# Half of the token tiles loaded in transposed form, their layer norm applied after the transposition by GpSimd, in a two-level fast matrix product

## Chip, core and metric

The kernel runs on one core of a Trainium2 chip. A core has TensorE (PE, matrix products into PSUM banks), VectorE (DVE), ScalarE (ACT), GpSimd (POOL) and SyncE (SP), which issues nearly all transfers here. Each engine takes its instructions in order; waits between engines are semaphores. The metric is the device time of one execution in microseconds (us).

## What is computed

2048 tokens of 512 features, two weight paths on the same normalised tokens, all float32:

```python
xn = (x - mean(x)) / sqrt(var(x) + eps)                  # per token
s  = xn @ (weight * block_mask).T                        # 512 -> 512
nx = xn * rsqrt(mean(xn**2) + eps) * ln_w
g  = silu( (silu(nx @ gate_w.T) * (nx @ up_w.T)) @ down_w.T )   # 512 -> 1792 -> 512
out = x + s * g
```

## The kernel before

**Two levels of a seven-product scheme.** Every matrix product is cut into 2 x 2 blocks twice, and at each level eight block products are replaced by seven, at the price of sums of blocks (Winograd's form of Strassen's scheme). For the first product the token operand B is xn transposed, features on the partitions: four chunks c of 128 features by four tiles t of 512 tokens. Chunk c = 2K + k and tile t = 2H + n, where (K, H) is the outer block and (k, n) the inner one. `raw[c, t]` is such a 128x512 tile. From the outer blocks come the seven outer operands q (`outer_b`):

- q = 1, 2, 3 are the blocks B(0,0), B(1,0), B(1,1) themselves,
- q = 5 is B(0,1) - B(0,0), q = 6 is B(1,1) minus operand 5, q = 7 is B(1,1) - B(0,1), q = 4 is B(1,0) minus operand 6.

`inner_b` makes four inner sums of each in the same way. The weight operand is cut and summed in parallel (`inner_a`, on GpSimd: four sums of 128x256 for the two first q of a group, four of 128x640 for the other five). There are eight weight groups: seven of gate and up columns and, as g = 7, the masked weight.

**Order by hand.** Every step is put down with `at(position, function, ...)`; at the end (L877) all are emitted in order of position. A position is one 128x512 product on TensorE, two records in the trace. An instance, one (g, q), has seven products and starts at 7j, j being its number; neighbouring instances overlap a little. First come q = 1 and 2 for all eight groups (positions 0 to 112): they need only tiles 0 and 1, the first half of the tokens. From position 112 on come the other five q of each group, which need tiles 2 and 3 too; after them the down projection (`down_instance`, L591). PSUM banks are shared out by letter: X (3), Y (2) and Z (1) for products, V (2) for everything else: transposes, gates, rows.

**The second half of the tokens**, in positions 14 to 82, beside the products of the first half:

- All four token tiles are loaded in natural form (tokens on the partitions, `load_x`) at the very start.
- `stats` (DVE, L125 and L126) takes mean and variance of each 128 tokens: tile 2 from position 14, tile 3 from 25.
- `factors` makes the scale and the bias per token, in three steps: DVE, a square root on ScalarE (L140), DVE (L136, L137). Those of tiles 2 and 3 stand at positions 36 to 38.5, beside those of `rms_factor`.
- `normalise` applies them in place: tile 3 on DVE (L146), tile 2 on ScalarE (L148).
- 32 TensorE transposes (`transpose`, L155) in eight batches of four, from position 51.5 for tile 3 and 65.5 for tile 2, into V banks.
- Chunks 2 and 3 (K = 1) are copied out by ScalarE (`evacuate`, L163). Chunks 0 and 1 (K = 0) stay in their bank and are read from there by DVE for the outer sums q = 5 and 7. DVE also makes q = 6; GpSimd makes q = 4, at positions 78 to 82.

**Queues.** SP issues its transfers in order of position as well: token loads, weight loads (`load_a`, `load_block`), stores of the hidden activations to `h_dram`, of partial sums to `acc_dram`. A transfer that must wait for its data holds back those behind it. Near the end `load_final` reads each tile of x transposed once more, for the residual sum.

The schedule of the steps named, in the kernel's own lines:

```python
    for t, p, step in ((0, T(7.1), 0), (1, T(12.5), 0), (2, 36.0, 1.2), (3, 36.1, 1.2)):
        plan(p, step, factors(t))
...
        at(14.0 + 2.5 * i, stats, 2, i)
        at(25.0 + 3 * i, stats, 3, i)
        at((44.0, 51.0, 55.2, 58.2)[i], normalise, 2, i, act)
        at(40.5 + 2.4 * i, normalise, 3, i, dve)
```

Of the kernel before, what the change touches and what calls it, by code (L numbers as in the profile page):

```python
# [8 lines left out]
F32 = mybir.dt.float32  # L9
I32 = mybir.dt.int32  # L10
AF = mybir.ActivationFunctionType
ALU = mybir.AluOpType
AX = mybir.AxisListType

P = 128
W = 512
# [15 lines left out]
def tile_masked_linear_gated_ffn(  # L32
# [11 lines left out]
    nc = tc.nc  # L44
    NT, H = x.shape
    KC = H // P
    G = gu.shape[0]
    NTT = NT // W
    TT = W // P
# [2 lines left out]
    h_dram = tc.dram_tile([7, G, 2, P, W], F32, name="h_dram")  # L52
    s_dram = tc.dram_tile([KC, NTT, P, W], F32, name="s_dram")
    rms_dram = tc.dram_tile([NT], F32, name="rms_dram")
    acc_dram = tc.dram_tile([G + 1, P, 4, W], F32, name="acc_dram")
    dw_dram = tc.dram_tile([4, P, G, 256], F32, name="dw_dram")

    const = ctx.enter_context(tc.tile_pool(name="const", bufs=1))
    small = ctx.enter_context(tc.tile_pool(name="small", bufs=2))
# [8 lines left out]
    def at(pos, fn, *args):  # L68
        events.append((pos, len(events), fn, args))
# [5 lines left out]
    mem = big.tile([P, sum(n for _, n in RINGS), W], F32, tag="mem", name="mem")  # L75
# [5 lines left out]
    F = first_slot  # L81

    def slot(tag, name=None):
        i, n = ring[tag]
        ring[tag][0] += 1
        return mem[:, first_slot[tag] + i % n, :]
# [6 lines left out]
    def bank(tag, name):  # L93
        return ps.tile([P, W], F32, tag=tag, name=name, bufs=PSB[tag])

    def add(eng, o, a, b, op=ALU.add):
        eng.tensor_tensor(o, a, b, op)  # L97

    dve, pool, act = nc.vector, nc.gpsimd, nc.scalar
# [3 lines left out]
    ident = const.tile([P, P], F32, tag="ident", name="ident")  # L103
# [9 lines left out]

    xt, raw, stat = {}, {}, {}
    agg = small.tile([P, NTT, TT, 2], F32, tag="agg", name="agg", bufs=1)
    rms = small.tile([P, NTT, TT], F32, tag="rms", name="rms", bufs=1)

    def load_x(t):
# [9 lines left out]
    def factors(t):  # L128


        scl = small.tile([P, TT], F32, tag="scl", name=f"scl_{t}")
        nb = small.tile([P, TT], F32, tag="nb", name=f"nb_{t}")
        stat[t] = (scl, nb)

        def last():
            nc.vector.reciprocal(scl, scl)  # L136
            nc.vector.scalar_tensor_tensor(nb, agg[:, t, :, 0], -1.0, scl, ALU.mult, ALU.mult)  # L137

        return [lambda: nc.vector.tensor_scalar(scl, agg[:, t, :, 1], 1.0 + EPS, EPS * EPS, ALU.mult, ALU.add),
                lambda: nc.scalar.activation(scl, scl, AF.Sqrt), last]  # L140
# [9 lines left out]
    pt = {}  # L150
# [17 lines left out]
    def rms_factor():  # L168

        def first():  # L170
            nc.vector.tensor_scalar_add(rms, agg[:, :, :, 1], EPS)
            nc.vector.reciprocal(rms, rms)
            nc.vector.tensor_mul(rms, agg[:, :, :, 1], rms)
            nc.vector.tensor_scalar_add(rms, rms, EPS)
        return [first, lambda: nc.scalar.activation(rms, rms, AF.Sqrt)]

    def rms_store():

        b = bank("V", "rms_rows")
        nc.tensor.transpose(b[: NTT * TT, :P], rms.rearrange("p t i -> p (t i)"), ident)  # L180
        rows = small.tile([NTT * TT, P], F32, tag="rms_rows", name="rms_rows", bufs=1)
        nc.vector.tensor_copy(rows, b[: NTT * TT, :P])
        nc.sync.dma_start(rms_dram.rearrange("(i p) -> i p", p=P), rows)

# [4 lines left out]
        nc.sync.dma_start(rms_bc[t], rms_dram[t * W : (t + 1) * W].unsqueeze(0).to_broadcast([P, W]))  # L189


    bblk, bop = {}, {}

    def outer_b(q, k, n, eng):


        B = lambda K, H_: pt[2 + n, k] if (K, H_) == (0, 1) else raw[2 * K + k, 2 * H_ + n]
        if q in (1, 2, 3):
            bblk[q, k, n] = B(*{1: (0, 0), 2: (1, 0), 3: (1, 1)}[q])
            return  # L200
        o = mem[:, F["free"], :] if (q, k, n) == (4, 0, 1) else slot("tmp" if (k, n) == (0, 1) else f"B{q}")
        a, b = {
            5: lambda: (B(0, 1), B(0, 0)),
            6: lambda: (B(1, 1), bblk[5, k, n]),
            7: lambda: (B(1, 1), B(0, 1)),
            4: lambda: (B(1, 0), bblk[6, k, n]),
        }[q]()
        add(eng, o, a, b, ALU.subtract)
        bblk[q, k, n] = o

    def inner_b(q, m, eng):
# [344 lines left out]
    fin, at_later = {}, []  # L556

    def load_final(R, Hh, i, slot_s, slot_x):
        r, n = divmod(i, 2)
        t, m = 2 * Hh + n, 2 * R + r  # L560
        fin[m, t] = mem[:, slot_s, :], mem[:, slot_x, :]
        nc.sync.dma_start(fin[m, t][0], s_dram[m, t])
        s_tile = fin[m, t][0]
        at_later.append(lambda: nc.gpsimd.tensor_tensor(s_tile, s_tile, rms_bc[t], ALU.mult))  # L564
        nc.sync.dma_start(fin[m, t][1], x_t[m * P : (m + 1) * P, t * W : (t + 1) * W])

    def finish(R, Hh, i, y, pos, eng, part=slice(0, W), source=None):
        r, n = divmod(i, 2)
# [108 lines left out]
    T = lambda us: (us - 14.0) / 0.86  # L677
# [17 lines left out]
    def plan(pos, step, todo):  # L695
        for i, fn in enumerate(todo):
            at(pos + step * i, fn)


    def warm(n, b):  # L700
        for _ in range(n):
            nc.tensor.matmul(b[:, :P], ident, ident, start=True, stop=True, skip_group_check=True)

    at(T(1.4), lambda: warm(26, bank("V", "idle")))
    for t, p, step in ((0, T(7.1), 0), (1, T(12.5), 0), (2, 36.0, 1.2), (3, 36.1, 1.2)):
        plan(p, step, factors(t))
    for i in range(TT):
        half = act if i < 2 else dve
# [16 lines left out]
    for q in (1, 2):  # L725
        for k in (0, 1):
            for n in (0, 1):
                at(8, outer_b, q, k, n, None)
    at(2.1, scale_a, 1, 0)
    at(5.2, scale_a, 1, 1)  # L730
    for i in range(TT):
        at(14.0 + 2.5 * i, stats, 2, i)
        at(25.0 + 3 * i, stats, 3, i)
        at((44.0, 51.0, 55.2, 58.2)[i], normalise, 2, i, act)
        at(40.5 + 2.4 * i, normalise, 3, i, dve)
    plan(36.2, 1.2, rms_factor())

    for t, p0 in ((3, 51.5), (2, 65.5)):
        n = t % 2
        for k, c in enumerate((2, 3, 0, 1)):  # L740
            for i in range(TT):
                at(p0 + 2 * k + 0.01 * i, transpose, t, c, i, "V")
            if c >= 2:
                at(p0 + 2 * k + 1.2, evacuate, t, c, act)
            else:
                at(p0 + 2 * k + 1.2, outer_b, 5, c, n, dve)
                at(p0 + 2 * k + 1.21, outer_b, 7, c, n, dve)
    for k in (0, 1):
        for n in (0, 1):
            at(72, outer_b, 3, k, n, None)  # L750
    for n, p0 in ((1, 60), (0, 74)):
        for k in (0, 1):
            at(p0 + 1.5 * k, outer_b, 6, k, n, dve)
            at(p0 + 2.2 + 1.7 * k + (16 if n == 1 else 4), outer_b, 4, k, n, pool)
    for q, p in ((6, 77), (5, 83), (4, 89), (7, 100), (3, 118)):
        for off, m, eng in ((0, 5, dve), (3, 6, dve), (5.5, 7, pool), (7.5, 4, pool)):
            at(p + off, inner_b, q, m, eng)
# [3 lines left out]
    for g in range(G + 1):  # L761
        p, rest = 7 * where[g, 1], 7 * where[g, BLOCKS[0]]
# [27 lines left out]
    for i, (R, K) in enumerate(QUADS):  # L790
        at(50, load_mask, R, K)
        at(62 + 3.5 * i, mask_rows, R, K)
    at(79.5, mask_blocks)
    at(120, rms_store)
    for t in range(NTT):
        at(END + 13, rms_rows, t)
# [51 lines left out]
    for (R, Hh), pos in (((0, 0), [D(0)(16)] * 4), ((1, 1), [D(2)(8)] * 4),  # L848
                         ((0, 1), [D(4)(20), D(4)(24), D(5)(3), D(5)(7)]),
                         ((1, 0), [D(5)(18), D(5)(22), D(6)(1), D(6)(5)])):  # L850
        for i, p in zip((0, 3, 1, 2), pos):
            at(p, load_final, R, Hh, i, fin_slots[0][i], fin_slots[1][i])
            at(p + 9, lambda: at_later.pop(0)())
# [71 lines left out]
```

## Time and profile before

| | us |
|---|---|
| median of three runs | 513.16 (512.6 to 513.7) |
| profiled execution | 513.17 |
| its span, first to last instruction | 511.4 |
| TensorE busy | 505.8 |
| VectorE busy | 380.4 |
| GpSimd busy | 340.9 |
| ScalarE busy | 182.6 |

The granted TensorE clock was 1.0 throughout. The mean traffic was 238 GB/s. In the stretch that the change touches, from 26 to 78 us, GpSimd is busy 11.5 us, VectorE 41.4 and ScalarE 34.3 of 52.

How to read it: a line of the table of groups or of an answer names the source line, the engine, the operation, its output and inputs, and then busy time, mean and waits. L97 is the line of a helper that makes every elementwise sum, so its groups are told apart by tiles and shapes. A line of waits reads "engine and line that waited <- what ended the wait: us in total, times, the longest". A line of a timeline reads "start, length, engine, line, operation, output<-inputs, shape, how many".

### The profile page before, as it was taken

To read this page: it belongs to the slowest core of one execution; us is meant where nothing else is said; L and a number is where in the kernel's file an instruction comes from. 1 tells how busy PE (TensorE), PEld (TensorE's weight loads), DVE (VectorE), ACT (ScalarE), POOL (GpSimd) and SP (SyncE) were. 2 spreads that over 40 slices of the span, in tenths; PEclk is the share of its full clock that TensorE was granted. 3 is DMA by queue.
4 is the path that set the end of the run, shared out by engine and by line. 5 is a ranking of instruction groups with operands and counts; after the bars stand their busy time and mean duration, and the time that the engine had idled before them with its cause. 6 is when DMAs were issued, how large, how long until landed. Compare 5 with 4: busy or idle time off the path is not lost. (4 is left out here: it accounts for less than half of the span.)

```text
span 511.4 us, 4943 instructions
## 1 busy us (share of the span) xinstructions
PE 505.8 (99%) x1269; PEld 231.8 (45%) x1269; DVE 380.4 (74%) x590; ACT 182.6 (36%) x348; POOL 340.9 (67%) x283
## 2 busy tenths in 40 slices
PE   8999999999999999999999999999999999999997
PEld 8444444444444444444444444444444444444444
DVE  6878689876977969699696978968747645367736
ACT  4656754633536353353634433330100101001111
POOL 5522224994795968869597789976662754739960
PEclk9999999999999999999999999999999999999999
DMA  8436636369159386785948667499997698476472
GB/s 289 164 132 238 247 133 227 135 236 350 48 219 348 147 302 228 238 289 208 338 166 294 209 239 254 169 332 383 357 339 270 204 374 327 146 252 216 151 229 83
DMA packets 60460, 121.59 MB, mean 238 GB/s; under 512 B 5760, under 2 KB 13328, under 8 KB 58384
## 3 DMA queue, kind: packets, MB, share of 16 engines
q1 hardware_dynamic: 60288, 121.27, 66.8%
q8 instruction: 10, 0.16, 0.1%
q14 instruction: 18, 0.15, 0.1%
q10 hardware_dynamic: 144, 0.00, 0.0%
HBM read 75.11 MB, written 46.15 MB: 237 GB/s over the span
## 5 line engine op out<-in xcount | busy, mean ns | idle before, releaser
L97 POOL TENSOR_TENSOR mem<-mem 128x512 f32<-128x512 f32 (+4 forms) x245 | 305.2, 1267 | 135.4 <-ACT mem L264 36.5
L343 PE MATMUL x<-mem 128*128 128x512 f32 x448 | 213.6, 595 | 0.2 <-DVE mem L97 0.2
L343 PEld LDWEIGHTS x<-mem 128*128 128x128 f32 x448 | 83.7, 190 | 107.3 <-issue 86.9
L97 DVE TENSOR_TENSOR mem<-x,mem 128x512 f32<-128x512 f32 x137 | 92.5, 684 | 42.0 <-PE x L343 41.1
L343 PE MATMUL y<-mem 128*128 128x512 f32 x224 | 114.5, 593 | 0.3 <-DVE mem L97 0.3
L97 DVE TENSOR_TENSOR mem<-mem 128x512 f32<-128x512 f32 (+3 forms) x60 | 74.7, 1252 | 7.8 <-PE dx L591 4.3
L591 PE MATMUL dx<-mem 128*128 128x512 f32 x174 | 78.3, 592 | 0.0
L97 DVE TENSOR_TENSOR mem<-y,mem 128x512 f32<-128x512 f32 x96 | 65.6, 684 | 9.8 <-PE y L343 8.5
L343 PEld LDWEIGHTS y<-mem 128*128 128x128 f32 x224 | 42.2, 190 | 53.0 <-issue 47.8
L350 ACT COPY z<-x 128x512 f32<-128x512 f32 x54 | 30.9, 573 | 97.9 <-PE x L343 92.2
L343 PE MATMUL z<-mem 128*128 128x512 f32 x112 | 57.3, 593 | 0.0
L591 PEld LDWEIGHTS dx<-mem 128*128 128x128 f32 x174 | 33.1, 190 | 41.6 <-issue 40.4
L591 PE MATMUL dy<-mem 128*128 128x512 f32 x98 | 44.5, 592 | 0.0
L409 ACT ACTIVATE gate<-mem 128x512 f32<-128x512 f32 x56 | 33.1, 601 | 25.3 <-DVE mem L97 20.9
L414 DVE TENSOR_TENSOR mem<-gate,mem 128x512 f32<-128x512 f32 x56 | 38.0, 681 | 5.1 <-POOL mem L97 4.3
L564 POOL TENSOR_TENSOR mem<-mem 128x512 f32<-128x512 f32 x16 | 25.0, 1570 | 15.3 <-DMA mem<-s_dram 15.2
L343 PEld LDWEIGHTS z<-mem 128*128 128x128 f32 x112 | 21.0, 190 | 24.9 <-issue 23.9
L574 ACT ACTIVATE silu<-mem 128x512 f32<-128x512 f32 x15 | 9.0, 602 | 64.6 <-DVE mem L97 48.3
L97 DVE TENSOR_TENSOR mem<-z,mem 128x512 f32<-128x512 f32 x41 | 28.0, 682 | 3.5 <-PE z L343 3.5
L591 PEld LDWEIGHTS dy<-mem 128*128 128x128 f32 x98 | 18.6, 190 | 23.4 <-issue 23.4
L97 DVE TENSOR_TENSOR mem<-dx,mem 128x512 f32<-128x512 f32 x16 | 11.0, 690 | 20.1 <-PE dx L591 20.1
L591 PE MATMUL dz<-mem 128*128 128x512 f32 x56 | 25.2, 592 | 0.0
(73 smaller groups left out, 289.2 us busy)
## 6 DMA issues: line engine op xcount, KB each, us to landing
h_dram<-mem SPq DMA_DIRECT2D x98, 256.0 KB, 2.1
mem<-h_dram SPq DMA_DIRECT2D x28, 768.0 KB, 6.2
mem<-in_gu SPq DMA_DIRECT2D x42, 256.0 KB, 3.7
acc_dram<-mem SPq DMA_DIRECT2D x8, 1024.0 KB, 4.2
mem<-acc_dram SPq DMA_DIRECT2D x8, 1024.0 KB, 6.7
mem<-in_x SPq DMA_DIRECT2D x16, 256.0 KB, 5.2
s_dram<-mem SPq DMA_DIRECT2D x16, 256.0 KB, 4.8
mem<-s_dram SPq DMA_DIRECT2D x16, 256.0 KB, 6.3
```

What stands on the lines that cost most here:

```text
L97: eng.tensor_tensor(o, a, b, op)
L343: nc.tensor.matmul(st[key], weights(g, q, m), operand(q, m), start=first and not (key == "z" and seeded), stop=True, skip_group_check=True)
L350: nc.scalar.copy(st["z"], st["x"])
L409: nc.scalar.activation(gate[key], t(), AF.Silu)
L414: nc.vector.tensor_mul(a(), gate[key], b())
L564: at_later.append(lambda: nc.gpsimd.tensor_tensor(s_tile, s_tile, rms_bc[t], ALU.mult))
L574: nc.scalar.activation(b[0][:, part], y[:, part] if source is None else source(), AF.Silu)
L591: nc.tensor.matmul(st[key], w(), b(), start=first and key != "z", stop=True, skip_group_check=True)
```

## The change

The tokens of tiles 2 and 3 are also read from `x_t`, a copy of the input that is already transposed and that the kernel's last stage reads before the change too. It is now laid out so that each 128x512 tile is contiguous. Tiles 2 and 3 in natural form stay loaded and serve the statistics only: their normalisation, their 32 transposes and the four evacuations are gone.

- `load_xt` loads the eight chunks, from position 21 on.
- The scale and the bias now run along the free dimension. `fac_rows` transposes the [128 tokens x 8] table of factors of a tile on TensorE into a V bank, ScalarE copies it to SBUF, SP stores it to DRAM and loads it back twice, as scale row and bias row over all 128 partitions. Tile 3's is at position 24.5 and tile 2's at 38.8.
- Tile 3's statistics and factors come first now (statistics from 14, factors at 22.6, 23.2 and 23.8); tile 2's statistics from 25, its factors as before.
- `scale_xt` is a GpSimd 128x512 operation in place: a multiplication by the scale row for all four chunks, and a sum with the bias row for chunks 2 and 3 alone. Chunks 0 and 1 (`u12`, K = 0) keep only the scale.
- The outer sums are rearranged so that the bias of B(0,1) is never needed: q = 7 is B(1,1) - B(0,1), taken before either has its bias (it cancels); q = 6 is operand 7 + B(0,0); q = 5 is B(1,1) minus operand 6; q = 4 is B(1,0) minus operand 6.
- For tile 3, GpSimd makes q = 7, 6 and 4 and DVE q = 5; for tile 2, GpSimd makes q = 4 and DVE the rest. All stand before position 73.

```diff
-    for t, p, step in ((0, T(7.1), 0), (1, T(12.5), 0), (2, 36.0, 1.2), (3, 36.1, 1.2)):
+    for t, p, step in ((0, T(7.1), 0), (1, T(12.5), 0), (3, 22.6, 0.6), (2, 36.0, 1.2)):
...
+    def load_xt(t, c):
+        K, k, n = c // 2, c % 2, t % 2
+        v = mem[:, F["v5"] + 4 + 2 * n + k, :] if K == 0 else slot("tmp" if (k, n) == (0, 1) else "B3")
+        (u12 if K == 0 else raw)[(k, n) if K == 0 else (c, t)] = v
+        nc.sync.dma_start(v, x_t[c, t])
+
+    def fac_rows(t):
+        b = bank("V", f"fac_rows_{t}")
+        nc.tensor.transpose(b[: 2 * TT, :P], fac[:, t - 2].rearrange("p f i -> p (f i)"), ident)
+        rows = small.tile([2 * TT, P], F32, tag="rows", name=f"fac_sb_{t}")
+        nc.scalar.copy(rows, b[: 2 * TT, :P])
+        nc.sync.dma_start(fac_dram[t - 2].rearrange("f (i p) -> (f i) p", p=P), rows)
+        for f in range(2):
+            fac_bc[t, f] = mem[:, F["B6"] + 3 + 2 * (t - 2) + f, :]
+            nc.sync.dma_start(fac_bc[t, f], fac_dram[t - 2, f].unsqueeze(0).to_broadcast([P, W]))
+
+    def scale_xt(t, c, f):
+        v = u12[c, t % 2] if c < 2 else raw[c, t]
+        add(pool, v, v, fac_bc[t, f], (ALU.mult, ALU.add)[f])
...
-            5: lambda: (B(0, 1), B(0, 0)),
-            6: lambda: (B(1, 1), bblk[5, k, n]),
-            7: lambda: (B(1, 1), B(0, 1)),
-            4: lambda: (B(1, 0), bblk[6, k, n]),
+            7: lambda: (B(1, 1), u12[k, n], ALU.subtract),
+            6: lambda: (bblk[7, k, n], B(0, 0), ALU.add),
+            5: lambda: (B(1, 1), bblk[6, k, n], ALU.subtract),
+            4: lambda: (B(1, 0), bblk[6, k, n], ALU.subtract),
...
-        at(14.0 + 2.5 * i, stats, 2, i)
-        at(25.0 + 3 * i, stats, 3, i)
-        at((44.0, 51.0, 55.2, 58.2)[i], normalise, 2, i, act)
-        at(40.5 + 2.4 * i, normalise, 3, i, dve)
+        at(14.0 + 2.5 * i, stats, 3, i)
+        at(25.0 + 3 * i, stats, 2, i)
...
-    for t, p0 in ((3, 51.5), (2, 65.5)):
-        n = t % 2
-        for k, c in enumerate((2, 3, 0, 1)):
-            for i in range(TT):
-                at(p0 + 2 * k + 0.01 * i, transpose, t, c, i, "V")
-            if c >= 2:
-                at(p0 + 2 * k + 1.2, evacuate, t, c, act)
-            else:
-                at(p0 + 2 * k + 1.2, outer_b, 5, c, n, dve)
-                at(p0 + 2 * k + 1.21, outer_b, 7, c, n, dve)
+    for k, (t, c) in enumerate((t, c) for t in (3, 2) for c in (0, 2, 1, 3)):
+        at(21.0 + 1.5 * k, load_xt, t, c)
+    at(24.5, fac_rows, 3)
+    at(38.8, fac_rows, 2)
+    for n, p0 in ((1, 31), (0, 56)):
+        t = 2 + n
+        for off, c, f in ((0, 0, 0), (1.5, 2, 0), (3, 1, 0), (4.5, 3, 0), (9, 2, 1), (10.5, 3, 1)):
+            at(p0 + off, scale_xt, t, c, f)
+        for off, q, k, eng in (((6, 7, 0, pool), (7.5, 7, 1, pool), (12, 6, 0, pool), (13.5, 6, 1, pool), (25.7, 5, 0, dve), (27.7, 5, 1, dve),
+                                (20, 4, 0, pool), (21.5, 4, 1, pool)) if n else
+                               ((6, 7, 0, dve), (8, 7, 1, dve), (11, 6, 0, dve), (12.5, 6, 1, dve), (14.7, 5, 0, dve), (16.7, 5, 1, dve),
+                                (15, 4, 0, pool), (16.5, 4, 1, pool))):
+            at(p0 + off, outer_b, q, k, n, eng)
...
-    for n, p0 in ((1, 60), (0, 74)):
-        for k in (0, 1):
-            at(p0 + 1.5 * k, outer_b, 6, k, n, dve)
-            at(p0 + 2.2 + 1.7 * k + (16 if n == 1 else 4), outer_b, 4, k, n, pool)
...
-        "x_t": x.reshape(B * S, H).T,
+        "x_t": x.reshape(-1, W, KC, P).transpose(2, 0, 3, 1),
```

More of the change, by code (lines that the diff above doesn't have):

```diff
@@ L54, in tile_masked_linear_gated_ffn @@
     rms_dram = tc.dram_tile([NT], F32, name="rms_dram")
+    fac_dram = tc.dram_tile([2, 2, W], F32, name="fac_dram")
     acc_dram = tc.dram_tile([G + 1, P, 4, W], F32, name="acc_dram")
@@ L115, in tile_masked_linear_gated_ffn @@
     agg = small.tile([P, NTT, TT, 2], F32, tag="agg", name="agg", bufs=1)
+    fac = small.tile([P, 2, 2, TT], F32, tag="fac", name="fac", bufs=1)
     rms = small.tile([P, NTT, TT], F32, tag="rms", name="rms", bufs=1)
@@ L128, in factors @@
     def factors(t):
-        scl = small.tile([P, TT], F32, tag="scl", name=f"scl_{t}")
-        nb = small.tile([P, TT], F32, tag="nb", name=f"nb_{t}")
+        if t < 2:
+            scl = small.tile([P, TT], F32, tag="scl", name=f"scl_{t}")
+            nb = small.tile([P, TT], F32, tag="nb", name=f"nb_{t}")
+        else:
+            scl, nb = fac[:, t - 2, 0, :], fac[:, t - 2, 1, :]
         stat[t] = (scl, nb)
@@ L180, in rms_store @@
         nc.tensor.transpose(b[: NTT * TT, :P], rms.rearrange("p t i -> p (t i)"), ident)
-        rows = small.tile([NTT * TT, P], F32, tag="rms_rows", name="rms_rows", bufs=1)
+        rows = small.tile([NTT * TT, P], F32, tag="rows", name="rms_rows")
         nc.vector.tensor_copy(rows, b[: NTT * TT, :P])
@@ L189, in rms_rows @@
         nc.sync.dma_start(rms_bc[t], rms_dram[t * W : (t + 1) * W].unsqueeze(0).to_broadcast([P, W]))
+    u12, fac_bc = {}, {}
+    def load_xt(t, c):
[15 more added lines that the diff above has]
+        add(pool, v, v, fac_bc[t, f], (ALU.mult, ALU.add)[f])
     bblk, bop = {}, {}
     def outer_b(q, k, n, eng):
-        B = lambda K, H_: pt[2 + n, k] if (K, H_) == (0, 1) else raw[2 * K + k, 2 * H_ + n]
+        B = lambda K, H_: raw[2 * K + k, 2 * H_ + n]
         if q in (1, 2, 3):
@@ L201, in outer_b @@
         o = mem[:, F["free"], :] if (q, k, n) == (4, 0, 1) else slot("tmp" if (k, n) == (0, 1) else f"B{q}")
-        a, b = {
-            5: lambda: (B(0, 1), B(0, 0)),
-            6: lambda: (B(1, 1), bblk[5, k, n]),
-            7: lambda: (B(1, 1), B(0, 1)),
-            4: lambda: (B(1, 0), bblk[6, k, n]),
+        a, b, op = {
+            7: lambda: (B(1, 1), u12[k, n], ALU.subtract),
+            6: lambda: (bblk[7, k, n], B(0, 0), ALU.add),
+            5: lambda: (B(1, 1), bblk[6, k, n], ALU.subtract),
+            4: lambda: (B(1, 0), bblk[6, k, n], ALU.subtract),
         }[q]()
-        add(eng, o, a, b, ALU.subtract)
+        add(eng, o, a, b, op)
         bblk[q, k, n] = o
@@ L564, in load_final @@
         at_later.append(lambda: nc.gpsimd.tensor_tensor(s_tile, s_tile, rms_bc[t], ALU.mult))
-        nc.sync.dma_start(fin[m, t][1], x_t[m * P : (m + 1) * P, t * W : (t + 1) * W])
+        nc.sync.dma_start(fin[m, t][1], x_t[m, t])
     def finish(R, Hh, i, y, pos, eng, part=slice(0, W), source=None):
@@ L731, in tile_masked_linear_gated_ffn @@
     for i in range(TT):
-        at(14.0 + 2.5 * i, stats, 2, i)
-        at(25.0 + 3 * i, stats, 3, i)
-        at((44.0, 51.0, 55.2, 58.2)[i], normalise, 2, i, act)
-        at(40.5 + 2.4 * i, normalise, 3, i, dve)
+        at(14.0 + 2.5 * i, stats, 3, i)
+        at(25.0 + 3 * i, stats, 2, i)
     plan(36.2, 1.2, rms_factor())
-    for t, p0 in ((3, 51.5), (2, 65.5)):
-        n = t % 2
-        for k, c in enumerate((2, 3, 0, 1)):
-            for i in range(TT):
-                at(p0 + 2 * k + 0.01 * i, transpose, t, c, i, "V")
-            if c >= 2:
-                at(p0 + 2 * k + 1.2, evacuate, t, c, act)
-            else:
-                at(p0 + 2 * k + 1.2, outer_b, 5, c, n, dve)
-                at(p0 + 2 * k + 1.21, outer_b, 7, c, n, dve)
+    for k, (t, c) in enumerate((t, c) for t in (3, 2) for c in (0, 2, 1, 3)):
[11 more added lines that the diff above has]
+            at(p0 + off, outer_b, q, k, n, eng)
     for k in (0, 1):
         for n in (0, 1):
-            at(72, outer_b, 3, k, n, None)
-    for n, p0 in ((1, 60), (0, 74)):
-        for k in (0, 1):
-            at(p0 + 1.5 * k, outer_b, 6, k, n, dve)
-            at(p0 + 2.2 + 1.7 * k + (16 if n == 1 else 4), outer_b, 4, k, n, pool)
+            at(73, outer_b, 3, k, n, None)
     for q, p in ((6, 77), (5, 83), (4, 89), (7, 100), (3, 118)):
```

## The prediction

> **What bounds the kernel now.** I read the page's busy table first, then TensorE's own waits, then stretches of the timelines around the change. The busy table:
>
> ```profile
> PE 505.8 (99%) x1269; PEld 231.8 (45%) x1269; DVE 380.4 (74%) x590; ACT 182.6 (36%) x348; POOL 340.9 (67%) x283
> ```
>
> A busy PE need not be PE at its peak, so I asked what TensorE ever waits for. The whole answer:
>
> ```profile
> PE idle L702 <- POOL ident masks.py:199: 1.3, 1, 1.3
> PE y L343 <- DVE mem L97: 0.3, 1, 0.3
> PE x L343 <- DVE mem L97: 0.2, 1, 0.2
> ```
>
> After its warm-up TensorE waits 0.5 us in two places. So an instruction removed from its queue shortens the run by what it takes in the queue, and every wait put into that queue lengthens it. What a transpose takes there comes from TensorE's timeline (start, length, records):
>
> ```profile
> 56.89 1.02 PE L343 MATMUL y<-mem 128*128 128x512 f32 x2
> 57.74 0.60 PE L155 MATMUL pt<-ident,mem 128*128 128x128 f32 x4
> 58.18 1.02 PE L343 MATMUL z<-mem 128*128 128x512 f32 x2
> 59.04 1.02 PE L343 MATMUL x<-mem 128*128 128x512 f32 x2
> 59.90 0.60 PE L155 MATMUL pt<-ident,mem 128*128 128x128 f32 x4
> 60.34 1.02 PE L343 MATMUL x<-mem 128*128 128x512 f32 x2
> ```
>
> Starts count, not lengths: one product (two records) takes 59.04 - 58.18 = 0.86 us, four transposes take 58.18 - 57.74 = 0.44 us, so one takes 0.109 us, though its record lasts 0.273. Position p of the schedule begins at 13.1 + 0.858p us up to position 50 (the z product of position 17 starts at 27.70, of 38 at 45.73).
>
> **What the Trainium skill says.** "TensorE: Matmul & The Clock Gate", Part 4 (PE-mode transpose), gives about 275 ns for a 128x128 transpose in a kernel. The record agrees (273), but back to back only 0.109 is taken, and that decides. "ScalarE: Activation LUTs", What ACT_TABLE_LOAD costs: a load of 1283 ns at every change of table set; the trace shows 1.28 at 32.84, 44.85 and 50.81. "SBUF — State Buffer", Who interferes with whom: a DVE instruction with two SBUF inputs contends with a GpSimd one that reads SBUF. The trace agrees: such a 128x512 DVE sum takes 0.68 us at 66.81 and 82.98, where GpSimd is idle, and a mean of 0.890 from 83 to 118 us, where GpSimd works throughout. "DMA: Bandwidth & Descriptors", Anatomy of one DMA: about 2.0 us fixed, mostly the write's receipt; the 256 KB stores to h_dram land in a median of 2.1, and the one small row store, at a busy moment, in 4.0.
>
> **Removed from TensorE.** 2 tiles x 4 chunks x 4 = 32 transposes x 0.109 = 3.49 us.
>
> **Added to TensorE.** Two small transposes, each with 128 moving columns like the one at L180 (same 273 ns record): 2 x 0.109 = 0.22 us. Each waits for its factors, and all products queue behind it.
>
> *Tile 3, position 24.5* (33.71 + 0.86 = 34.57 us). The statistics of tile 3 take the places that tile 2's had; the last ends at 32.91 on DVE. Then one small DVE operation (about 0.16), the square root on ScalarE (0.2, just after the z copy at 32.25, which ends at 32.82), DVE's x sum (waits for TensorE until about 33.1, ends 33.75), and the reciprocal and the bias row (0.36): ready at about 34.15. No stall, 0.4 us to spare. Nor is there another table load: Sqrt is loaded at 1.16 us and the next load, for Silu, comes only after this position:
>
> ```profile
> 32.25 0.57 ACT L350 COPY z<-x 128x512 f32<-128x512 f32 x1 [0.70 <-PE x L343]
> 32.84 1.28 ACT L409 ACT_TABLE_LOAD   x1
> 34.13 1.12 ACT L409 ACTIVATE gate<-mem 128x512 f32<-128x512 f32 x2
> 36.49 0.58 ACT L371 COPY mem<-x 128x512 f32<-128x512 f32 x1 [1.23 <-PE x L343]
> ```
>
> That load now queues behind the row copy (about 34.95 to 35.25), so the two gates end at about 37.65 instead of 35.25. ScalarE's next copy starts at 37.65 and its z copy at 38.2 is on time. DVE's gate products, at 36.51 before, slip by 0.6; DVE has 0.5 + 0.2 us of idle time at 42.0 and 43.2, so it is level again by 43. Cost zero while these gaps stand, up to 0.7 if not.
>
> *Tile 2, position 38.8.* Its factors keep their places, so their times can be read, from ScalarE's and DVE's timelines:
>
> ```profile
> 44.85 1.28 ACT L140 ACT_TABLE_LOAD   x1
> 46.15 0.30 ACT L140 ACTIVATE scl<-scl 128x4 f32<-128x4 f32 x2
> ...
> 46.58 0.69 DVE L97 TENSOR_TENSOR mem<-y,mem 128x512 f32<-128x512 f32 x1
> 47.19 0.17 DVE L136 RECIPROCAL scl<-scl 128x4 f32<-128x4 f32 x1
> 47.39 0.16 DVE L137 SCALAR_TENSOR_TENSOR nb<-agg,scl 128x4 f32<-128x4 f32 x1
> ```
>
> The bias row is done at 47.55; without tile 3's share of the small operations, 47.4. TensorE is through position 38 at 46.59 + 0.11 = 46.70. With 0.09 for the weight load, it stands for 0.8 us, a wait that nothing later gives back. Bounds: 0 (DVE 0.8 earlier) and 1.7 (DVE still carrying its lag of about 1 us).
>
> **DVE and ScalarE.** DVE loses 4 normalisations (0.54) and 12 outer sums (0.68), 10.3 us, and gets 8 sums of 0.68 to 0.89, 5.4 to 7.1. ScalarE loses 4 normalisations (0.81) and 4 evacuations (0.58), 5.6, and gets two copies of about 0.3. Both hidden under TensorE before as well: nothing.
>
> **GpSimd and the queue of transfers.** GpSimd gets 12 operations for tile 3 and 8 for tile 2, at 1.27 to 1.33 us (its 128x512 sums at 121.11 and 124.74; 1.412 in the stretch 83 to 118), minus 4 that move here from after position 78: 16 x 1.3 = 21 us more. It is busy only 11.5 of the 52 us from 26 to 78, so there is room, but its queue is in order: behind the first scale stand the weight sums for group 3, due on TensorE at positions 44, 46, 48 and 50 (50.9, 52.5, 54.3, 56.0 us). SP's chain: row copy 35.25, store issued (0.37), landed about 37.7, two broadcasts issued (0.4 each), landed about 41.2. From there, in order of position, with 1.3 and 0.76: three scales to 45.1, first weight sum 45.9, second 47.9, third 50.0, fourth 50.8. Each is 4 us or more early. Counted on in the same way, group 4's weight sums end at 58.1, 58.8, 60.9 and 61.6 us (due at 63.9, 65.6, 67.3 and 69.0) and tile 3's last operation at 62.9. Tile 2's scales run 62.9 to 68.1; DVE asks for them at positions 62 and 64 (67.3 and 69.0). Cost zero, with 0.9 us to spare at the last.
>
> On SP, the waits for two small stores (about 2 us each) hold back the other token chunks, the h_dram stores of group 0 (37.2 to about 39.7; their buffer is written again near 47), the acc_dram stores and the weight loads behind them, which have 2 us or more to spare. Eight more loads and four broadcasts, 3 MB, fall into 31 to 54 us, where the DMA engines are 53% busy. Nothing. The contiguous x_t loads are hidden now and stay so.
>
> **Sum**, against the profiled execution, 513.17 us (span 511.4 and 1.77 around it; the runs' median is 513.16): 513.17 - 3.49 + 0.22 + 0.8 = **510.7 us**, 2.5 us or 0.5% less.
>
> **Rivals.**
> 1. *No stall at tile 2's row*: DVE is ahead because statistics and sums moved. 513.17 - 3.27 = 509.9. For: TensorE is the only resource in short supply. Against: the square root alone ends at 46.45 and DVE is busy until 47.2.
> 2. *The gain is waited away*: further on DVE or GpSimd set the pace, or the first row also stalls (0.4 to spare is little). About 511.6 to 514. For: the chain of waits runs through DVE and GpSimd from 312.6 to 326.1 us, where TensorE waits its 0.2. Against: from 112 to 326 us GpSimd is busy 173.0 and DVE 172.3 of 214, and GpSimd waits there mostly for what TensorE and ScalarE produce, so their work moves up with it.
> 3. *Slower: GpSimd's backlog reaches DVE's queue.* If the rows land as slowly as the later ones (4.0 for the store, 6.1 for the broadcasts), GpSimd starts at 46.4 instead of 41.2; at the busy stretch's rates (1.41, 0.90) the 12 operations and eight weight sums then take 24.1 us and tile 2's four scales another 5.6: they end at 76.1, not 68.1. DVE stands at position 64 (69.0) for 7.1 us, its evacuations behind it; some 1.7 us are slack (the shortest: an x snapshot planned at 7j + 5, its bank needed at 7j + 8, three positions less the sum's 0.69 and a little for the wait), 5.4 reach TensorE, and the net is 513.2 - 2.5 + 5.4 = 516. It turns slower than before once the last scale ends later than 69.0 + 1.7 + 2.5 = 73.2 us. For: both rows pass one in-order queue, with a wait for the store between. Against: DMA is quiet at 35 us, and in 26 to 78 us DVE has mostly PSUM inputs, with GpSimd's 128x256 sums at 0.729 there.
>
> **How the numbers follow.** Forecast 0.55 (510.0 to 511.6), rival 1 0.13, rival 2 0.18 of which 0.10 still ends below 512.1 and 0.08 within 0.2%, rival 3 0.14. Faster 0.55 + 0.13 + 0.10 = 0.78; same 0.08; slower 0.14. A difference of 0.2%, 1.0 us, is about what a measurement can tell from none. The range 509.6 to 513.2 takes in rival 1 and most of rival 2, and leaves out rival 3.
>
> **What will show it.** TensorE has 32 fewer L155 records, and position 112 is about 2.5 us earlier. TensorE's waits name DVE's factors once, near 46.7 us, for 0.8. No table load is added. GpSimd starts scaling near 41 and ends tile 2's four scales near 68. It is wrong if TensorE waits for GpSimd's weight sums between 50 and 70 us, or DVE waits for GpSimd at 67 to 76.

## The result, and the profile after

The changed kernel takes 514.95 us (median of 16 runs, 513.07 to 519.08) against 513.35 for the kernel before (16 runs): a ratio of 1.0028 with a 95% interval from 1.0011 to 1.0044. It was forecast at 510.7 and faster; it is slower, by about as much as a measurement can tell. The runs fall into two groups: six lie at 513.07 to 513.56 us, all with a mean granted TensorE clock of 1.000; nine lie at 514.84 to 515.61 with 0.997, and one at 519.08 with 0.993. The profiled execution is one of the nine: 515.29 us, span 513.5.

The busy table of the changed kernel:

```profile
PE 504.2 (98%) x1239; PEld 228.5 (44%) x1239; DVE 382.1 (74%) x582; ACT 177.8 (35%) x342; POOL 364.1 (71%) x299
```

TensorE has 30 records fewer (32 transposes gone, two added) and GpSimd 23 us more (21 forecast). DVE, which was to lose 3 to 5 us, has 1.7 more. TensorE's waits (us in total, times, longest):

```profile
PE fac_rows L208 <- DVE fac L142: 2.0, 1, 2.0
...
PE x L372 <- DVE mem L98: 0.9, 1, 0.9
...
```

Two waits that the kernel before didn't have: one for tile 2's row, one for a DVE sum. (The lines left out have two small ones more, 0.4 and 0.2 us at 15 us, for transposes of the first half of the tokens; they stand ahead of everything that was changed on TensorE, and the run with the row later, below, has none of them.) TensorE's timeline at the first of them (start, length, records):

```profile
46.04 1.02 PE L372 MATMUL z<-mem 128*128 128x512 f32 x2
49.04 0.27 PE L208 MATMUL fac_rows<-ident,fac 128*8 128x128 f32 x1 [1.98 <-DVE fac L142]
49.15 2.67 PE L372 MATMUL x<-mem 128*128 128x512 f32 x4
51.60 1.92 PE L372 MATMUL y<-mem 128*128 128x512 f32 x2
53.31 1.99 PE L372 MATMUL x<-mem 128*128 128x512 f32 x4
55.14 1.02 PE L372 MATMUL y<-mem 128*128 128x512 f32 x2
```

The z product is through at 46.90 and the row starts at 49.04: 2.14 us, where 0.8 was forecast. After it the products are slow. The y product of 51.60 takes 1.71 us until the next start, twice 0.86. From 49.15 to the z product of 55.99 there are six products in 6.84 us, where six take 5.15: 1.69 us lost. The granted clock in the windows around it (stretch and its length, busy times and records of TensorE, its weight loads, DVE, ScalarE and GpSimd, then the clock, DMA share, GB/s):

```profile
47.00:49.00 2.00, 0.06 (x1) 0.00 (x0) 1.86 (x6) 0.21 (x1) 2.00 (x4) 1.00 1.03 397
49.00:51.00 2.00, 1.96 (x5) 0.98 (x6) 1.27 (x2) 0.25 (x1) 2.00 (x3) 0.78 0.78 297
51.00:53.30 2.30, 2.30 (x3) 0.77 (x3) 0.00 (x0) 0.58 (x1) 2.30 (x3) 0.50 0.28 93
```

In finer windows the clock is 1.00 from the row to 50.1 us, 0.50 from 50.1 to 53.5, and 1.00 again after that. So it halves about 1 us after the products go on, and 3.4 us at half speed are the 1.7 us lost. Why the row was late is on DVE's timeline:

```profile
44.93 0.24 DVE L144 TENSOR_SCALAR fac<-agg 128x4 f32<-128x4 f32 x1
45.09 0.16 DVE L176 TENSOR_SCALAR rms<-agg 128x16 f32<-128x16 f32 x1
45.28 0.25 DVE L177 RECIPROCAL rms<-rms 128x16 f32<-128x16 f32 x1
45.57 0.83 DVE L178 TENSOR_TENSOR rms<-agg,rms 128x16 f32<-128x16 f32 x1
46.44 0.65 DVE L179 TENSOR_SCALAR rms<-rms 128x16 f32<-128x16 f32 x1
...
48.39 0.17 DVE L141 RECIPROCAL fac<-fac 128x4 f32<-128x4 f32 x1
48.59 0.39 DVE L142 SCALAR_TENSOR_TENSOR fac<-agg,fac 128x4 f32<-128x4 f32 x1
```

In the kernel before the same three operations (product and sum of the root mean square, and the bias row) took 0.34, 0.17 and 0.16 us; here 0.83, 0.65 and 0.39, 1.2 us more. They handle 16 or 4 elements per partition. The first two in the kernel before:

```profile
45.33 0.34 DVE L173 TENSOR_TENSOR rms<-agg,rms 128x16 f32<-128x16 f32 x1
45.71 0.17 DVE L174 TENSOR_SCALAR rms<-rms 128x16 f32<-128x16 f32 x1
```

What is new beside them is GpSimd, which works from 40.1 to 55.8 us on tile 3's scales and sums, with group 3's weight sums in between. The GpSimd instructions that ran when the three operations of the changed kernel started:

```profile
45.10 1.27 POOL L98 TENSOR_TENSOR mem<-mem 128x512 f32<-128x512 f32 x1
46.33 0.72 POOL L98 TENSOR_TENSOR mem<-mem 128x256 f32<-128x256 f32 x1
48.24 0.72 POOL L98 TENSOR_TENSOR mem<-mem 128x256 f32<-128x256 f32 x1
```

They end at 46.37, 47.05 and 48.96 us, and the three DVE operations at 46.40, 47.09 and 48.98. Each is held until the GpSimd instruction that it found running is through: a scale in the first case, a weight sum in the other two. In the kernel before, the weight sums ran from 44.10 to 47.15. The product was held by one of them (ends at 45.67 and 45.64), the sum began 0.01 us ahead of the next one and was not, and the bias row came when GpSimd was idle. So the new work acts in two ways: by its own instructions, and by moving the weight sums, behind it in GpSimd's queue, to other times.

**The books of the profiled execution.** Against 513.17: transposes gone -3.49, two rows +0.22, the wait for the row +2.14, half clock +1.69, the second wait +1.05 (80.89 + 0.86 = 81.75 to 82.80), 0.2 in the first microseconds (position 24 starts at 33.91 instead of 33.71, ahead of anything changed on TensorE). Sum +1.81; measured +2.12. Without the half clock the same sum gives 513.3, which is where the six runs with clock 1.000 lie. Nearly all of it is lost in the first 117 us: TensorE starts its 113th 128x512 product at 116.60 us instead of 114.70.

### The profile page after: what moved, and what is told of

Its sections match the earlier page's. It is cut to its first block, busy times and chain, and to the rows that moved or that the text cites. A ratio compares the mean times of both kernels' runs of the same rounds, so it can differ in the third digit from the quotient of the medians.

```text
span 513.5 us, 4900 instructions
## 1 busy us (share of the span) xinstructions
PE 504.2 (98%) x1239; PEld 228.5 (44%) x1239; DVE 382.1 (74%) x582; ACT 177.8 (35%) x342; POOL 364.1 (71%) x299
## 5 line engine op out<-in xcount | busy, mean ns | idle before, releaser
L98 POOL TENSOR_TENSOR mem<-mem 128x512 f32<-128x512 f32 (+4 forms) x261 | 326.9, 1275 | 114.3 <-ACT mem L400 30.0
L98 DVE TENSOR_TENSOR mem<-mem 128x512 f32<-128x512 f32 (+2 forms) x64 | 82.5, 1292 | 7.4 <-PE dx L620 4.4
L98 DVE TENSOR_TENSOR mem<-y,mem 128x512 f32<-128x512 f32 x96 | 65.8, 685 | 11.0 <-PE y L372 9.7
L372 PEld LDWEIGHTS y<-mem 128*128 128x128 f32 x224 | 42.7, 191 | 54.5 <-issue 49.5
L620 PEld LDWEIGHTS dy<-mem 128*128 128x128 f32 x98 | 18.6, 190 | 23.4 <-issue 23.2
```

The lines of the kernel that those rows point to most:

```text
L372: nc.tensor.matmul(st[key], weights(g, q, m), operand(q, m), start=first and not (key == "z" and seeded), stop=True, skip_group_check=True)
L620: nc.tensor.matmul(st[key], w(), b(), start=first and key != "z", stop=True, skip_group_check=True)
```

## The experiments

**Theory 1**: the loss is the wait for tile 2's row and the clock after it; the wait is long because GpSimd's new operations and DVE share access to SBUF and stretch the small DVE operations ahead of the row. **Rival 1**: DVE and GpSimd are behind anyway, and the waits only show it; take one away and it comes back later. **Rival 2**: the lower clock has nothing to do with the wait. **Rival 3**: the second wait is one late sum, not a backlog. (These three are explanations of the result; the prediction's rivals have numbers of their own.) Each run is compared with the kernel before on the same chip (513.1 to 513.3 us).

**The row later.** One position altered in the changed kernel:

```diff
-    at(38.8, fac_rows, 2)
+    at(42.2, fac_rows, 2)
```

> The changed kernel, with one position altered: the factor row of tile 2 goes through TensorE at position 42.2 instead of 38.8. Theory 1 (the loss is TensorE's wait for that row, 2.1 us, and the lower granted clock after it, 1.7 us in the profiled execution): the factors are ready at 48.9 us, position 42.2 is reached at about 49.7, so both vanish; clock 1.000 in every execution, about 511.2 us, 2.1 below the kernel before. Rival 1 (DVE and GpSimd are behind by then, and the wait only gives them time): TensorE then waits for DVE or GpSimd sums between 60 and 90 us instead, the wait of 0.9 at 82 us grows to 3 or more, and the time stays at 513 to 515.

511.56 us, ratio 0.9968 (0.9955 to 0.998). No wait for the row, full clock until the last product, and the second wait unchanged. TensorE's waits:

```profile
...
PE x L372 <- DVE mem L98: 0.9, 1, 0.9
...
```

Theory 1 holds for the row and the clock, and rival 1 falls: nothing came back, and the 113th product starts at 112.29 us. The mean clock of 0.998 or 0.999 that this run too lists lies behind the last product (0.80 from 506 us on in its profile).

**The root mean square later.**

```diff
-    plan(36.2, 1.2, rms_factor())
+    plan(38.5, 1.2, rms_factor())
```

> The changed kernel, with the five steps of the root mean square moved behind tile 2's factors (positions 38.5 and 39.7 instead of 36.2 and 37.4). Theory 1: these four small DVE operations took 1.9 us in the changed kernel (0.9 in the kernel before) ahead of the factors on DVE, so the factors are ready at about 47.2 us and TensorE waits 0.3 to 0.6 us instead of 2.1; clock 1.000, 511.4 to 511.8 us. Rival 1: 513 to 515 us, as the wait moves to 60 to 90 us.

511.94 us over 8 runs from 510.45 to 512.69, ratio 0.9968 (0.9956 to 0.998). The profiled execution is one of the four slower ones, 512.61 us. Its wait was 1.3 us, not 0.3 to 0.6: with the root mean square out of the way, the bias row itself met a GpSimd operation. DVE's timeline:

```profile
46.73 1.25 DVE L142 SCALAR_TENSOR_TENSOR fac<-agg,fac 128x4 f32<-128x4 f32 x1
```

0.16 us of work took 1.25, about the length of the GpSimd operation beside it (46.70 to 47.96; the bias row ends at 47.98). After this wait of 1.3 us the products went on at 0.86.

**The row alone, without GpSimd's work.** In the kernel before, tile 2's factors are put side by side and transposed into a bank that nobody reads (the main line of the edit):

```diff
+    at(38.8, lambda: nc.tensor.transpose(bank("V", "fac_rows")[: 2 * TT, :P], fac.rearrange("p f i -> p (f i)"), ident))
```

> The kernel before, with one thing added: at position 38.8 TensorE transposes tile 2's eight factor columns into a V bank that nobody reads. This is the new row's wait alone, without GpSimd's new work. Theory 1: DVE has the factors at 47.55 us as in the kernel before, TensorE waits 1.0 us, 0.1 for the transpose: 514.4 us. If GpSimd's work is what made it 2.1 in the changed kernel, it stays at 1.0 here; if DVE's order alone did, it is 2.1 here too. Whether a wait of 1.0 lowers the clock is open; if it does, 516.

514.52 us, ratio 1.0023 (1.0013 to 1.0032). DVE and then TensorE:

```profile
45.78 0.34 DVE L177 TENSOR_TENSOR rms<-agg,rms 128x16 f32<-128x16 f32 x1
46.15 0.17 DVE L178 TENSOR_SCALAR rms<-rms 128x16 f32<-128x16 f32 x1
...
48.14 0.27 PE L741 MATMUL fac_rows<-ident,fac 128*8 128x128 f32 x1 [0.95 <-DVE scl L140]
```

This is the wait as it was forecast: 0.95 us, small operations at their old length, clock 0.999 or 1.000 in all nine runs.

**The same, with the wait drawn out** by two unused statistics operations on DVE ahead of the factors:

```diff
+    def hold():
+        for _ in range(2):
+            st = small.tile([P, 6], F32, tag="st", name="st_hold")
+            nc.vector.bn_stats(st, xt[2, 0])
+    at(38.39, hold)
```

> As the run with the short pause, and two statistics operations of 0.6 us each (results unused) ahead of the factors on DVE, so that TensorE's wait is about 2.2 us as in the changed kernel. Theory 1: 513.35 + 2.3 = 515.7 us while the clock stays 1.000, and 517.3 in the executions in which the pause lowers the granted clock for some 6 us to 0.7; both kinds are seen, as in the changed kernel. Rival 2 (the lower clock comes from the changed kernel's own mixture of work or from chance, not from the pause): clock 1.000 in every execution, 515.7 us.

517.22 us, ratio 1.007 (1.0058 to 1.0083). Four of five runs are at 516.66 to 517.67 us with a clock of 0.995 to 0.997, one at 516.04 with 1.000. The wait was 2.1 us; the windows after it:

```profile
49.20:51.00 1.80, 1.79 (x4) 0.78 (x5) 0.75 (x2) 0.00 (x0) 0.00 (x0) 0.58 0.00 0
51.00:52.60 1.60, 1.60 (x4) 0.56 (x3) 1.15 (x2) 0.00 (x0) 0.00 (x0) 0.50 0.00 0
```

Rival 2 falls: the kernel before, with a wait of that length and no new work on GpSimd or in the transfers, shows the same half clock and the same two groups. The clock falls to 0.50 for 3.4 us (49.5 to 52.9), not to 0.7 for some 6 us.

**The transposes twice**, in the kernel before: the line that issues them stands there a second time.

> The kernel before with each of the 32 transposes of tiles 2 and 3 issued twice into the same place. Theory 1: 32 x 0.109 = 3.5 us more on TensorE, 516.8 us. If the record's length counted (0.273), 522; if the transposes were hidden behind other waits, 513.3.

516.58 us against 513.23, +3.35 (2.7 to 4.2 by the interval), ratio 1.0068 (1.0053 to 1.0082). 32 transposes are worth 3.5 us by their starts, not 8.7 by their records; that term of the sum was right.

**GpSimd's work alone.** The kernel before with the unread row, and ten products on scratch tiles (the lines of the products):

```diff
+    u, v = mem[:, F["v5"] + 4, :], mem[:, F["v5"] + 5, :]
+    at(20, lambda: nc.gpsimd.memset(mem[:, F["v5"] + 4 : F["v5"] + 6, :], 0.5))
+    for p in (31, 32.5, 34, 35.5, 37, 38.5, 40, 41.5, 43, 44.5):
+        at(p, lambda: add(pool, u, u, v, ALU.mult))
```

> The run with the short pause (the kernel before and tile 2's row, read by nobody), and ten 128x512 GpSimd products on scratch tiles at positions 31 to 44.5, whose results nobody reads. Theory 1: GpSimd's work alone stretches the small DVE operations ahead of the factors, so that TensorE's wait grows from 0.95 to 1.5 to 2.2 us; 514.5 becomes 515 to 516, or 517 in executions whose clock falls. If the sharing of SBUF between DVE and GpSimd is not the cause, the wait stays at 0.95 and the time at 514.5.

519.34 us, ratio 1.0126 (1.0112 to 1.014), all four runs with a clock of 0.992 to 0.997. The wait grew not to 2 but to 4.0 us. DVE:

```profile
45.20 1.24 DVE L175 TENSOR_SCALAR rms<-agg 128x16 f32<-128x16 f32 x1
46.48 0.25 DVE L176 RECIPROCAL rms<-rms 128x16 f32<-128x16 f32 x1
46.77 0.36 DVE L177 TENSOR_TENSOR rms<-agg,rms 128x16 f32<-128x16 f32 x1
47.16 1.18 DVE L178 TENSOR_SCALAR rms<-rms 128x16 f32<-128x16 f32 x1
...
49.85 1.07 DVE L141 SCALAR_TENSOR_TENSOR fac<-agg,fac 128x4 f32<-128x4 f32 x1
```

Three operations of 0.16 us each lose about 1 us apiece. They end at 46.44, 48.34 and 50.92, the GpSimd instructions beside them at 46.41, 48.31 and 50.90. Only the size was missed, and why it varies can be read: each small operation loses up to one GpSimd operation, depending on where in it it falls.

**The changed kernel without that work.** `scale_xt` returns at once, and operands 6 and 7 of tile 3 are set to `B(1, 1)`, so this kernel leaves out the layer norm of tiles 2 and 3. The weight sums stay, at their old times.

> The changed kernel without GpSimd's new work for the factors: the scale and the bias of tiles 2 and 3 are not applied, and operands 6 and 7 of tile 3 are put equal to its B(1,1), so that layer norm of the second half of the tokens is left out; all rows, loads, the row's position 38.8 and DVE's sums stay. Theory 1: the wait for the row is 0.9 us as in the run with the short pause, the clock stays at 1.000, DVE's sums take 0.68 us and the wait near 82 us is gone: 513.3 - 3.27 + 0.95 = 511.0 us. If GpSimd's work is not the cause: wait 2.0, 0.9 near 82, 513.3 to 515.

511.07 us, ratio 0.9959 (0.9944 to 0.9974). TensorE's waits:

```profile
PE fac_rows L208 <- DVE fac L142: 0.9, 1, 0.9
...
PE x L375 <- DVE mem L98: 0.2, 1, 0.2
```

The forecast's own sum, with 513.3 us for the kernel before and a wait of 0.95 us in place of 0.8, gives 511.0. So what the prediction missed hangs on the GpSimd work taken out here. The 0.2 is that of the kernel before.

**GpSimd's work for tile 3 later**, from position 43 instead of 31, so that it starts behind the weight sums of group 3.

> The changed kernel, with all of tile 3's GpSimd work 12 positions later (from 43 instead of 31), so that it stands behind the weight sums for group 3 and begins near 47 us, when tile 2's factors are nearly through. The row stays at position 38.8. Theory 1: the small DVE operations ahead of the factors take 0.9 us again as in the kernel before, TensorE waits 0.9 to 1.2 us instead of 2.0, and the clock stays at 1.000. If GpSimd's operations are not what held DVE up, the wait is 2.0 again and the clock falls in most executions. The total is no test here: tile 2's sums now come late, and TensorE's second wait near 82 us grows from 0.9 by 0 to 3 us; 512 to 515.

521.52 us, ratio 1.0155 (1.014 to 1.0169). Half a hit. The operations up to 47.5 us are short again (0.41 and 0.17), but tile 3's first scale then begins and meets the bias row:

```profile
47.78 1.00 DVE L142 SCALAR_TENSOR_TENSOR fac<-agg,fac 128x4 f32<-128x4 f32 x1
```

The wait is 1.7 us instead of 0.9 to 1.2; the products after it keep 0.86. The late scales then make TensorE wait 6.2 us for DVE, 3.8 of it at once, after which the clock halves as well.

**DVE's load between 64 and 90 us.** The row at 42.2; tile 3's q = 5 sums and the mask sums earlier:

```diff
...
-(25.7, 5, 0, dve), (27.7, 5, 1, dve)
+(20.2, 5, 0, dve), (22.2, 5, 1, dve)
...
-        at(50, load_mask, R, K)
-        at(62 + 3.5 * i, mask_rows, R, K)
+        at(45, load_mask, R, K)
+        at(51.5 + 2.2 * i, mask_rows, R, K)
```

> The run with the row later, and six DVE operations out of the stretch 64 to 90 us, in which DVE was busy 25.5 of 25.6 us: tile 3's two q = 5 sums at positions 51.2 and 53.2 instead of 56.7 and 58.7, the four mask sums at 51.5 to 58.1 instead of 62 to 72.5 (their loads at 45 instead of 50). Theory 1: TensorE's wait of 0.9 us near 77 us is DVE's backlog there, made of its sums that GpSimd's operations stretch from 0.68 to a mean of 1.2 us; with six operations fewer it vanishes, about 510.7 us. Rival 3: the wait is due to one sum that is due at one moment, not to a backlog; it stays at 0.9, 511.5 us.

512.87 us, ratio 0.9998 (0.999 to 1.0006): a miss. The profiled execution, 514.05 us, is one of three at 514.05 to 514.84; the other eleven lie at 512.33 to 513.06 and may wait less or elsewhere. In it the wait near 77 us is gone, but TensorE's waits for DVE now come at 48.8 (1.4 us), 52.0, 62.8 and 65.8 (1.1):

```profile
PE x L372 <- DVE mem L98: 2.7, 3, 1.4
```

The moved sums fell beside GpSimd's again and took 1.74 and 1.34 us, and the waits at 62.8 and 65.8 come behind them. The wait at 48.8 is the small operations once more: two of the root mean square took 1.32 and 1.18 in this execution, and the x sum behind them came late. Nothing edited in this run stands ahead of them on DVE, so this part is put down to how they happen to fall; that is not shown. Neither theory 1 nor rival 3 had that right.

**Both later**: the row at 42.2 and the root mean square at 38.5.

> The changed kernel with both later: the row of tile 2 at position 42.2 and the steps of the root mean square at 38.5 and 39.7. Theory 1: TensorE waits neither for the row nor for an x sum behind stretched small operations; the wait of about 0.9 us near 77 us stays. 511.2 us, clock 1.000 up to the last product. Rival 1: the waits come back between 60 and 90 us, 512.5 or more.

511.45 us, ratio 0.9967 (0.9955 to 0.998), clock 1.000 in all five runs. The wait near 77 us is not there in the profiled execution; one of 0.8 us is, at 51.6, behind a root mean square operation of 1.31. The DVE sum just ahead of the late x sum, 1.80 us in the changed kernel, took 1.78 here too, without a wait; the three two-input sums ahead of it took 0.67, 0.67 and 0.70 us instead of 1.05, 0.68 and 1.24. So one stretched sum alone does not make the second wait, which speaks against rival 3.

**And the mask sums in DVE's idle time**, their loads at the start:

```diff
-        at(50, load_mask, R, K)
-        at(62 + 3.5 * i, mask_rows, R, K)
+        at(2, load_mask, R, K)
+        at(43.2 + 2.4 * i, mask_rows, R, K)
```

> As the run with both later, and the four mask reductions (0.67 us each on DVE, one input in SBUF, 0.67 in every run so far) at positions 43.2 to 50.4, where DVE is idle a third of the time, with their loads at position 2, where the DMA engines rest from 18.7 to 24 us. Theory 1: DVE's backlog between 64 and 85 us shrinks by 2.7 us and TensorE's wait of 0.9 near 77 us vanishes: 510.4 us. Rival 3: the wait stays at 0.9 or moves a few us: 511.2.

510.97 us (510.8 to 511.65), ratio 0.9961 (0.9948 to 0.9973), 2.1 us below the kernel before. In the profiled execution, 511.65 us and the slowest of the five, the wait near 77 us is absent and one of 0.6 at 51.7 remains. Against the run without this edit the difference, 0.5 us, is no more than those five runs spread. This version and three others (the row later, the root mean square later, both later) beat both kernels.

## Why the prediction was wrong

- **The transposes' worth** was right: 3.49 forecast, 3.35 measured by doubling them.
- **Tile 3's row** was right: ready at 34.25, 34.15 forecast, no wait. No table load was added, and the gate products slipped to 37.28 and were made up.
- **Tile 2's row is the step that failed.** The prediction said: "Its factors keep their places, so their times can be read". The places are the same and the times are not. It priced the contention of DVE and GpSimd for 128x512 sums, from the skill and from a measured mean of 0.890 us, and left it out for operations of 0.16 us that stand ahead of a TensorE instruction. GpSimd's new work, and the weight sums that it moved, lengthened them by 1.2 us; the wait became 2.1 us instead of the 0.8 forecast. Without that work it is 0.85 to 0.95 (the row alone, and the changed kernel without GpSimd's work): the rest of the step was sound.
- **The clock was in no term and in no rival.** A wait was priced at its length. One of about 2 us also costs 1.7 us of half clock, in 10 of 16 runs here by their times and mean clocks (one of them was profiled); this puts the median beyond the range, which otherwise would just have missed it (513.3 against an upper end of 513.2).
- **DVE's sums, "nothing".** The eight new sums were put at 5.4 to 7.1 us. In the changed kernel they took 1.51, 1.15, 1.16, 1.05, 0.68, 1.24, 1.80 and 0.68, 9.3 us, since GpSimd ran without a break from 60.6 to 81.6. DVE was full from 66 to 91 us, and TensorE waited 0.9 to 1.05 us at 82.
- **The prediction's rival 2** had the outcome of the six full-clock runs (513.07 to 513.56, within its 511.6 to 514): the gain is waited away. It looked for the waits at the first row and after 112 us; they came at the second row and at 82.
- **The prediction's rival 3** named the wrong way from GpSimd to TensorE. DVE never stood waiting for tile 2's scales; it was slowed by the sharing of SBUF. GpSimd's start, 40.1 us, was earlier than the 41.2 forecast. Its last scale for tile 2 ended at 72.2 us, as it stood idle until 60.6 for weights that ScalarE, behind TensorE's wait, was late with; with the row later it ended at 68.1, as forecast.

What stays open: why a wait of this length halves the clock in some runs and not in others, and how to tell from a schedule which small operations will be held. In the traces it is a matter of which of two instructions starts first, by hundredths of a microsecond.

## What to carry to other kernels

When work is added to GpSimd, ask which DVE operations will run beside it, and reprice the short ones too: an operation of 0.16 us on a path to TensorE can cost a whole GpSimd operation, and old work in GpSimd's queue moves to new times. Put an instruction that depends on such a path later in TensorE's queue than the arithmetic says; here 3.4 positions of slack turned a loss of 1.6 us into a gain of 1.7. And price a wait on a saturated TensorE from about 2 us on above its length.

## What the runs showed of the hardware

- **Short DVE operations are held until GpSimd's instruction is through.** With GpSimd busy on 128x512 operations, a tensor_scalar of 128x16 went from 0.16 or 0.17 to 1.18 to 1.32 us and the bias row (two SBUF inputs, 128x4) from 0.16 to as much as 1.25. Reciprocals, batch statistics, mask reductions and sums with a PSUM input kept their lengths (0.17 or 0.25, 0.68, 0.67, 0.68 us) in the same stretches. That sums with two SBUF inputs contend and those with a PSUM input don't is what "SBUF — State Buffer", Who interferes with whom, says; it also lists tensor_scalar, in a two-port mode. GpSimd's 128x256 weight sums, 0.73 us long, hold the same operations for less: 0.65 us for the tensor_scalar in the changed kernel. In the 13 profiled executions, all 54 tensor_scalar, tensor_tensor and scalar_tensor_tensor operations of 128x16 or 128x4 between 28 and 60 us that took over 0.22 us end 0.02 to 0.03 us after a GpSimd instruction does. One that starts 0.01 us ahead of a GpSimd instruction keeps its length (0.17 at 45.71 us in the kernel before, at 45.93 without GpSimd's new work, and at 46.10 with it later).
- **About 2 us without a product can halve TensorE's clock.** "TensorE: Matmul & The Clock Gate", Why this matters for your kernels, warns of gaps beyond about 3 us. Here 2.0 and 2.1 us did it in most runs, and after 0.85 to 1.7 us the products went on at 0.86. In the four profiled executions that show it, after waits of 2.0, 2.1, 3.8 and 4.0 us, the clock is 0.50 for 3.4 us each time, from 0.3 to 1.1 us after the products go on. So the loss was about 1.7 us, whatever the length of the wait.
